# A graph layer on one core: slots ranked ahead, other segment lengths, a step's hand-overs moved, and a shorter last softplus

## The chip, the cores and the metric

The kernel runs on one core of one Trainium2 chip. Its time is that of one launch on the device, in microseconds, as the median of several runs. A core has five engines that run their own instruction streams in order and wait for each other through semaphores: TensorE (matmul, PE in the profile, its weight loads PEld), VectorE (DVE), ScalarE (ACT), GpSimd (POOL) and SyncE (SP), whose queue issues most of the transfers here.

## The reference

12,500 nodes with 128 features; 412,500 edges, sorted by their target `dst`, each with 20 edge attributes and a weight `rcut`. Layer norm and ReLU on the nodes, then one message-passing layer, then a residual:

```python
h = jnp.maximum(_layernorm(x, axis=-1), 0.0)
# the layer, with f_ij = edge_attr_20, rcut_ij = edge_weight, idx_i = src, idx_j = dst
h = h @ W_in2f
Wij = ssp(f_ij @ W_f1 + b_f1) @ W_f2 + b_f2        # ssp(x) = softplus(x) - log 2
Wij = Wij * rcut_ij[:, None]
x_ij = h[idx_j] * Wij
agg = jax.ops.segment_sum(x_ij, idx_i, num_segments=12500)
out = x + ssp(agg @ W_o1 + b_o1) @ W_o2 + b_o2
```

So rows of `h` are gathered by `dst`, which is sorted, and summed by `src`, which is not.

## The kernel before

Edges are taken in 806 chunks of 512, four chunks to a group, 202 groups. One step `k` of the main loop works on several chunks at once, and the code writes each engine's order out by hand (`tc.manual_schedule()`); the function `step` is that order. For a chunk there are these parts:

- `rows`: a window of 32 rows of `h`, split into three bf16 parts, is loaded (`near`), at a row number read from memory. It needs the rows of `h` to have been stored: they are made by `make_h`, four node tiles of 128 at a time (a quad), and the first quads are made ahead of and during the first steps.
- `hidden`, `hidden_log`, `hidden_end`: for a pair of chunks, the first matmul to `z` in PSUM, then softplus as Abs, Exp and Ln on ScalarE and a maximum-and-add on VectorE (L668), to `r`.
- `window`, `pick`, `picked`: a comparison builds a selection matrix `at` (L744), matmuls with `near` give the gathered rows (L772), and ScalarE scales them by `rcut` to `hg` (L780).
- `bias`, `value`: ScalarE writes the bias to `v` in PSUM (L757) and four f32 matmuls add `r @ wf2` to it (L764).
- `message`: VectorE multiplies `v` and `hg` into `o` (L791), and GpSimd issues four indirect DMAs (scatters) of 128 rows each (L795), to the slots found for these edges. `o` has four buffers of two chunks.
- `blocks`, `rank`, `rank_end`: the slots. A table in HBM has, for every block of 128 nodes, `T` tiles of 128 slots (one more in a part of the blocks); a running count in PSUM (`free`, L692 and L725) and a maximum over it (L697) give each edge a free slot of its block. This is done six chunks ahead (`LR`).

The edges are cut into segments, each with a table of its own, whose slots are cleared by DMA first (L1099). When a segment's edges are all scattered, it is collected: class `Collect` goes over the blocks in units of up to `UT` tiles, loads a unit (`m`, L833), compares places with slots (`to`, L844), sums by matmul into a PSUM bank `acc` (L857) and adds four blocks at a time to `agg` in SBUF (L880, `keep`). The collecting of all segments but the last is spread over the steps by a planner: a due time for each, and a rate of tiles a step, until six steps beyond the last chunk. The last segment is collected after the loop. With it the result is made for four blocks at a time (a node quad, 25 in all) by `finish`: `agg @ wo1` to PSUM (L414), softplus with Abs, Relu, Exp, Ln on ScalarE (L385 and others) and an addition on VectorE (L420), the bias added to the residual `xo` (L423), `@ wo2` (L427), the last addition (L431), and a store (L434).

Of the kernel before, what the change touches and what calls it, by code (L numbers as in the profile page):

```python
# [9 lines left out]
F32 = mybir.dt.float32  # L10
# [12 lines left out]
SEGS = (88, 40, 30, 14, 14, 8, 8)  # L23
# [6 lines left out]
UT = 6  # L30
# [11 lines left out]
def gnn_kernel(  # L42
# [38 lines left out]
    class Segment:  # L81
# [4 lines left out]
        def __init__(self, k):  # L86
# [7 lines left out]
            mean = (SEGS[k] * TG * P - (own[1] - own[0])) / QT * P / N  # L94
# [32 lines left out]


    tables = [(0, QN)]
# [4 lines left out]
    for c in range(NC):  # L134
        n = c * CH * N // n_edges
        table_of.append(0 if n < QN - NEAR - P else min(n // QN, NQ - 1) + 1)
# [4 lines left out]
    bf1, nbf1, bo1 = (sbuf(n, [P, 1]) for n in ("bf1", "nbf1", "bo1"))  # L141
# [10 lines left out]
    bf12 = sbuf("bf12", [P, P])  # L152
    zero = sbuf("zero", [P, ZR * RW])
# [27 lines left out]
    def load_x(q):  # L181
        n = min(QT, NTILE - q * QT)
        full = min(n, N // P - q * QT)
        xb = ln.tile([P, QT, P], F32, name="xb")
        if full < n:
            nc.vector.memset(xb[:, full:n, :], 0.0)
            nc.sync.dma_start(xb[:N % P, full, :], x[q * QN + full * P:N, :])
        if full:
            nc.sync.dma_start(xb[:, :full, :], x[q * QN:q * QN + full * P, :]
                              .rearrange("(c p) f -> p c f", p=P))  # L190
        return xb
# [59 lines left out]

    def constants():
# [3 lines left out]
        first_load(0)  # L256
        nc.sync.dma_start(win, w_in2f)

        for j in range(NCHUNK):
            nc.sync.dma_start(wf1[32 * j:32 * j + RBF, :], w_f1)  # L260

        nc.scalar.preload_act_table_set("natural_log_exp_and_others")
        nc.scalar.dma_start(bf1, b_f1[:, None])
        nc.scalar.dma_start(wf2, w_f2)
        nc.scalar.dma_start(bf2, b_f2[None, :].to_broadcast([P, P]))
        make_identity(nc, ident)
        for _ in bounds(0, nc.gpsimd):
            pass

        prow_i = early_room[:WP, rows_at + 5 * NC:rows_at + 5 * NC + 1].bitcast(I32)  # L270
# [6 lines left out]
                                pattern=[[1, P]], channel_multiplier=-1)  # L277
        nc.gpsimd.memset(zero, 0.0)
# [8 lines left out]
        nc.vector.memset(bad, 0.0)  # L287
        nc.vector.memset(rel[:, NPART - 1, :], 0.0)
        nc.vector.memset(ones, 1.0)
        nc.vector.memset(none, 0.0)  # L290

        for t in range(QT):
            nc.vector.memset(turn[:, :, t:t + 1], -1.0 if t % 2 else 1.0)
        nc.vector.tensor_scalar(prow_i, prow_i, 7, None, op0=ALU.logical_shift_right)
        nc.vector.tensor_copy(prow, prow_i)
# [3 lines left out]

    def biases(psum):  # L300

        nc.vector.tensor_scalar(nbf1, bf1, -1.0, None, op0=ALU.mult)
        b12 = psum.tile([P, QT, P], F32, name="b12", tag="acc")[:, 0, :]
        nc.tensor.matmul(b12, bf1.to_broadcast([P, P]), wf2, start=True, stop=True)
        nc.vector.tensor_add(bf12, b12, bf2)

    def late_loads():
        nc.sync.dma_start(wo1, w_o1)
        nc.sync.dma_start(wo2, w_o2)
        nc.sync.dma_start(bo1, b_o1[:, None])  # L310
        nc.sync.dma_start(bo2, b_o2[None, :].to_broadcast([P, P]))

    early = {}
    quads = []


    def make_h(q, psum):

        n = min(QT, NTILE - q * QT)
        xb = early.pop(q, None)  # L320
        if xb is None:
            xb = load_x(q)
            for _ in range(3):
                yield
# [39 lines left out]
        for (b, rows), table in zip(tables, h3_t):  # L364
            lo = max(0, b - q * QN) // P
            hi = min(n, (b + rows - q * QN) // P)
            if lo < hi:
                r = q * QN + lo * P - b
# [3 lines left out]
                if b + rows == QN:  # L372
                    yield
            if q == NQ - 1:
# [4 lines left out]
            h3[q * QN:q * QN + n * P, :].rearrange("(c p) f -> p c f", p=P),  # L379
            hb[:, :n, :, :].rearrange("p c k f -> p c (k f)"))  # L380
        yield
# [15 lines left out]
    def finish(t0, n, sT, quad, psum):  # L397
# [13 lines left out]
        yield  # L411

        z = psum.tile([P, 2, CH], F32, name="z_out", tag="z")[:, 0, :n * P]
# [3 lines left out]
        softplus_parts(a_n, r_n, z, bo1)  # L417
        softplus_logs(a_n)
        yield
        nc.vector.tensor_add(r_n, r_n, a_n)  # L420
        for p, cs, rows in pieces:
            xi = xo[:p, cs, :]
            nc.vector.tensor_add(xi, xi, spread(bo2[:p, :], xi.shape[1]))  # L423
        yield
        v = psum.tile([P, QT, P], F32, name="v_out", tag="v", bufs=3)
# [92 lines left out]
    with tc.tile_pool(name="edge", bufs=2) as edge, tc.tile_pool(  # L518
# [46 lines left out]
        class Group:  # L565


            def __init__(self, g):
# [3 lines left out]
                if g % NB == 0:  # L572
                    f = edge.tile([P, NB, CH], F32, name="f")
                    for j in range(NCHUNK):
                        nc.sync.dma_start(f[32 * j:32 * j + RBF, :, :],
                                          f_t[g:g + NB, j].rearrange("b k n -> k b n"))
                    kept["f"] = f
                self.f = kept["f"][:, g % NB, :]
                i = g - self.seg.g0
                if i % SB == 0:  # L580
                    w = min(SB, ceil_div(self.seg.c1, NCHUNK) - g) * TG
                    cols = slice(g * TG, g * TG + w)
                    src_i = edge.tile([P, SB * TG], I32, name="src_i")
                    nc.sync.dma_start(src_i[:, :w], src_t[:, cols])
                    rcut = edge.tile([P, SB * TG], F32, name="rcut")
                    nc.sync.dma_start(rcut[:, :w], rcut_t[:, cols])
                    kept["cols"] = [w, src_i, rcut]
                self.cols = kept["cols"]
                self.at = slice(i % SB * TG, (i % SB + 1) * TG)
                if g == 0:  # L590
                    rel_store(0)
                self.rel = edge.tile([WP, NCHUNK, CH], BF16, name="rel", bufs=4)
                nc.sync.dma_start(self.rel, rel_d[g * NCHUNK:(g + 1) * NCHUNK, :][None, :, :]
                                  .to_broadcast([WP, NCHUNK, CH]))
                self.inb = {}
                self.pair = {}
                self.near = {}

            def rows(self, c):

                k = self.g * NCHUNK + c
                t = table_of[k]
                i = int(k >= FIRST)
                at = k - heads[i].start
                self.near[c] = edge.tile([WP, P], BF16, name="near", bufs=8)
                start = nc.sync.value_load(shifts[i][0:1, at:at + 1], min_val=0,
                                           max_val=tables[t][1] - WR)
                nc.sync.dma_start(self.near[c], h3_t[t][bass.ds(start, WR), :]
                                  .rearrange("r (k f) -> (r k) f", f=P))

            def columns(self):
                if len(self.cols) == 3:
                    w, src_i, _ = self.cols
# [7 lines left out]
                    place = edge.tile([P, SB * TG], F32, name="place")  # L621
                    nc.vector.tensor_copy(place[:, :w], src_i[:, :w])

# [22 lines left out]
                self.rcut, self.blk, self.place, self.start = (t[:, self.at] for t in self.cols[2:])  # L646

            def hidden(self, c):

                z = psum.tile([P, 2, CH], F32, name="z")  # L650
                for k in range(2):
                    rows = slice(32 * (c + k), 32 * (c + k) + RBF)
                    nc.tensor.matmul(z[:, k, :], wf1[rows, :], self.f[rows, :],  # L653
                                     start=True, stop=True)
                a = quad.tile([P, 2, CH], F32, name="a", bufs=2)
                nc.scalar.activation(a, z, AF.Abs, bias=bf1)  # L656
                nc.scalar.activation(a, a, AF.Exp, scale=-1.0)  # L657
                self.pair[c] = z, a

            def hidden_log(self, c):  # L660
                _, a = self.pair[c]
                nc.scalar.activation(a, a, AF.Ln, bias=half, scale=0.5)  # L662

            def hidden_end(self, c):

                z, a = self.pair[c]
                r = quad.tile([P, 2, CH], F32, name="r")
                nc.vector.scalar_tensor_tensor(r, z, nbf1, a, op0=ALU.max, op1=ALU.add)  # L668
                self.pair[c] = r

            def blocks(self, c):
                inb = quad.tile([P, QT, NBLK], F16, name="inb")
# [6 lines left out]
            def rank(self, c):  # L679

                seg = self.seg
                if c == 0:
                    self.top = edge.tile([P, TG], F32, name="top")
                    self.slot = edge.tile([P, TG], I32, name="slot", bufs=4)
# [11 lines left out]
            def rank_end(self, c):  # L696
# [16 lines left out]
                if c == self.n - 1 or self.g == 0:  # L713

                    w = slice(c * QT if self.g == 0 else 0, (c + 1) * QT)
# [24 lines left out]

            def window(self, c):
# [6 lines left out]
            def bias(self, c):  # L748


                v = psum.tile([P, QT, P], F32, name="v", bufs=3)
                if self.g * NCHUNK + c < 2:
                    nc.tensor.matmul(v.rearrange("p t f -> p (t f)"),
# [458 lines left out]
```

## Time and profile before

| | |
|---|---|
| median of 3 runs | 4226.62 us (4223.92 to 4229.81) |
| the profiled execution itself | 5772.48 us |
| its span | 5770.8 us |
| mean granted TensorE clock | 0.718 |
| busy: PE, PEld, DVE, ACT, POOL | 67%, 50%, 59%, 47%, 54% |
| first scatter, start of the last scatter | 29.44 us, 5625.94 us |
| DMA | 820.8 MB, mean 142 GB/s |

The profiled execution is 37% longer than a run without the recorder. In rows of the trace the start comes first, then the duration in us, the engine, the line, the operation with output and inputs, and in brackets the idle time ahead of it and what ended it. In rows of groups the count, the busy time and the mean ns of one follow the names. In rows by stretch the engines follow as PE, PEld, DVE, ACT, POOL, then the granted clock, the DMA share and GB/s. PEclk among the slices is the granted clock in tenths.

### The profile page before, as it was taken

How to read it: one execution, taken by the hardware profiler on the slowest of the kernel's cores; microseconds unless marked ns; L12 is line 12 of the kernel's file. 1: busy time of each engine (PE TensorE's matmuls, PEld its weight loads, DVE VectorE, ACT ScalarE, POOL GpSimd, SP SyncE). 2: the span in 40 equal slices, each digit the busy share in tenths (PEclk: the TensorE clock that was granted, in tenths of full speed). 3: DMA queues.
4: the chain of work that ended last, by engine and by line, in shares of the span. 5: the costliest groups of instructions: out<-in, count | busy, mean ns of one | idle time of the engine just before them, and what ended most of it. 6: DMA issues, size and time to landing. Idle time of an engine off the chain costs nothing. (4 is left out here: it accounts for less than half of the span.)

```text
span 5770.8 us, 71871 instructions
## 1 busy us (share of the span) xinstructions
PE 3877.3 (67%) x21576; PEld 2912.2 (50%) x21576; DVE 3382.9 (59%) x6726; ACT 2715.3 (47%) x5490; POOL 3103.5 (54%) x3244
## 2 busy tenths in 40 slices
PE   5556555556555555577777777777777777777778
PEld 3333333333333333356655666566566665655557
DVE  5555555555444444466665666666666666566767
ACT  4455554555444444444444444444444444444444
POOL 5555555555555555555555555555555555555550
PEclk7665566565556566578777787788877788787879
DMA  5444443343333333255664554655555555555547
GB/s 150 138 135 141 130 141 119 115 137 104 99 89 87 106 109 87 82 152 161 188 183 137 158 160 144 190 163 157 160 168 173 154 150 178 165 141 153 145 126 215
DMA packets 515581, 820.80 MB, mean 142 GB/s; under 512 B 177074, under 2 KB 312870, under 8 KB 515186
## 3 DMA queue, kind: packets, MB, share of 16 engines
q1 hardware_dynamic: 411586, 602.85, 37.4%
q0 software_dynamic: 103168, 213.15, 11.2%
q8 instruction: 176, 2.88, 0.2%
q14 instruction: 219, 1.79, 0.1%
q10 hardware_dynamic: 432, 0.13, 0.0%
HBM read 419.09 MB, written 396.64 MB: 141 GB/s over the span
## 5 line engine op out<-in xcount | busy, mean ns | idle before, releaser
L795 POOL DMA_INDIRECT slots<-o,slot x3224 | 3100.3, 962 | 2522.6 <-DVE o L791 1605.2
L764 PE MATMUL v<-wf,r 128*128 128x128 f32 x6448 | 1209.4, 345 | 527.4 <-ACT a L657 207.3
L857 PEld LDWEIGHTS acc<-to,m 128*128 128x128 f32 x8132 | 1249.1, 238 | 577.1 <-issue 280.8
L857 PE MATMUL acc<-to,m 128*128 128x128 f32 x8132 | 1342.0, 329 | 271.0 <-DVE agg L880 136.4
L764 PEld LDWEIGHTS v<-wf,r 128*128 128x128 f32 x6448 | 1077.6, 251 | 850.7 <-issue 301.8
L780 ACT ACTIVATE hg<-picked,rcut 128x128 f32<-128x128 f32 x3224 | 913.1, 365 | 1256.6 <-remote 801.2
L697 DVE TENSOR_REDUCE top<-free 128x4 f32<-128x392 f32 x806 | 451.5, 560 | 1650.5 <-remote 990.2
L757 ACT ACTIVATE v<-bf 128x512 f32<-128x512 f32 x804 | 478.0, 595 | 1212.9 <-DVE o L791 888.5
L653 PE MATMUL z<-f,wf 20*128 20x512 f32 x1612 | 661.1, 881 | 406.9 <-DVE r L668 242.4
L844 DVE TENSOR_TENSOR to<-count_ps,m 128x512 f32<-128x512 f32 (+3 forms) x824 | 644.7, 806 | 255.3 <-remote 109.3
L772 PE MATMUL picked<-near,at 96*128 96x128 bf16 x3224 | 398.5, 257 | 495.3 <-ACT hg L780 317.4
L668 DVE SCALAR_TENSOR_TENSOR r<-z,nbf,a 128x1024 f32<-128x1024 f32 x403 | 516.2, 1281 | 242.3 <-ACT a L662 136.3
L656 ACT ACTIVATE a<-z,bf 128x1024 f32<-128x1024 f32 x403 | 454.0, 1127 | 400.4 <-remote 267.8
L772 PEld LDWEIGHTS <-at 96*128 96x128 bf16 x3224 | 315.5, 118 | 558.1 <-issue 531.3
L791 DVE TENSOR_TENSOR o<-v,hg 128x512 f32<-128x512 f32 x806 | 547.8, 680 | 16.8 <-ACT hg L780 12.8
L744 DVE TENSOR_TENSOR at<-count_ps,rel 96x512 bf16<-96x512 f32 x806 | 545.3, 677 | 0.0
L653 PEld LDWEIGHTS z<-f,wf 20*128 20x128 f32 x1612 | 174.6, 241 | 620.9 <-issue 428.9
L662 ACT ACTIVATE a<-a,half 128x1024 f32<-128x1024 f32 x403 | 468.1, 1162 | 0.0
L673 DVE TENSOR_TENSOR inb<-count_ps,blk 128x392 f16<-128x392 f32 x806 | 445.9, 554 | 0.0
L657 ACT ACTIVATE a<-a 128x1024 f32<-128x1024 f32 x403 | 425.8, 1057 | 12.8
L725 PE MATMUL free<-inb,rest_of 128*128 128x392 f16 x806 | 335.3, 416 | 117.6 <-issue 46.9
L692 PE MATMUL free<-inb,after 128*128 128x392 f16 x806 | 335.9, 417 | 17.4 <-issue 13.6
(108 smaller groups left out, 1142.5 us busy)
## 6 DMA issues: line engine op xcount, KB each, us to landing
m<-slots SPq DMA_DIRECT2D x311, 387.0 KB
m<-slots SPq DMA_DIRECT2D x317, 258.0 KB
rel<-rel_d SPq DMA_DIRECT2D x202, 384.0 KB
m<-slots SPq DMA_DIRECT2D x172, 322.5 KB
slots<-o,slot POOLq DMA_INDIRECT x3224
slots<-zero SPq DMA_DIRECT2D x96, 387.0 KB
slots<-zero SPq DMA_DIRECT2D x64, 516.0 KB
f<-in_f_t SPq DMA_DIRECT2D x404, 80.0 KB
```

The costliest lines, as they stand in the source:

```text
L653: nc.tensor.matmul(z[:, k, :], wf1[rows, :], self.f[rows, :], start=True, stop=True)
L662: nc.scalar.activation(a, a, AF.Ln, bias=half, scale=0.5)
L668: nc.vector.scalar_tensor_tensor(r, z, nbf1, a, op0=ALU.max, op1=ALU.add)
L744: nc.vector.tensor_tensor(at, prow_ps.to_broadcast([WP, CH]), self.rel[:, c, :], op=ALU.is_equal)
L757: nc.scalar.activation(v, spread(bf12, QT), AF.Copy)
L764: nc.tensor.matmul(v[:, i, :], r[:, i * P:(i + 1) * P], wf2, start=False, stop=True, skip_group_check=True)
L772: nc.tensor.matmul(ps[:, i, :], at[:, i * P:(i + 1) * P], near, start=i == 0, stop=i == QT - 1, skip_group_check=True)
L780: nc.scalar.activation(hg[:, i, :], ps[:, i, :], AF.Copy, scale=self.rcut[:, j:j + 1])
L791: nc.vector.tensor_mul(o[:, :, :P], v, hg)
L795: put = nc.gpsimd.indirect_dma_start(out=views[j % VIEWS], out_offset=bass.IndirectOffsetOnAxis(ap=self.slot[:, j:j + 1], axis=0), in_=o[: ...
L844: nc.vector.tensor_tensor(to[:, :n, :], count_ps[:, None, :].to_broadcast([P, n, P]), self.m[u][:, :n, P:].to_broadcast([P, n, P]), op=ALU ...
L857: nc.tensor.matmul(self.acc[b // QT][:, i, :], m[:, j, :P], to[:, j, :], start=t == 0, stop=t == self.seg.tiles(b) - 1)
```

## The change

- **Slots ahead.** What finds the slots leaves `Group` for a class `Places`. The lead of the ranks over the step ramps over 20 steps to 6, and from step 100 on grows by one every four steps to 64. In the last 64 steps no ranks are left, and the PSUM bank of the counts then serves as a second bank for the sums.
- **Segments.** Nine instead of seven; the last three have 3, 3 and 4 groups, so that one tile a block is enough for them. Units have up to 4 tiles (`UT`), `m` nine buffers. The planner counts 3.3 tiles more for the end of each quad and lets the last 64 steps take 1.3 times the work.
- **Hand-overs.** The order in a step is rewritten: the message goes first, the result of a rank is read a step later, picks are made two chunks ahead from step 18 on, Abs and Exp stand with Ln in the next step, the sums of a unit are added a step later, the sums of a quad are kept at several places of a step.
- **Bias.** The bias goes to `v` by a fifth matmul, from three bf16 parts of it, behind the four; `v` has one buffer, `picked` two, where both shared three.
- **First tile alone.** `make_h` takes tile 0, then tiles 1 to 3, then quads; a table of 128 rows serves the first chunks. Constants and small loads are put in another order.
- **Last softplus.** Abs, Exp and Ln; then one VectorE operation takes the maximum with `z` from PSUM and adds. The bias on `xo` is added by GpSimd. `bo1` is folded into `bo2` through a matmul made earlier.

The core of the diff:

```diff
-SEGS = (88, 40, 30, 14, 14, 8, 8)
+SEGS = (88, 41, 25, 18, 12, 8, 3, 3, 4)
+LEAD = 64
-UT = 6
+UT = 4
...
-            mean = (SEGS[k] * TG * P - (own[1] - own[0])) / QT * P / N
+            edges = min(n_edges, self.c1 * CH) - self.c0 * CH
+            mean = (edges - (own[1] - own[0])) / QT * P / N
...
+    made_h = [(0, 1), (1, QT - 1)]
+    made_h += [(t, min(QT, NTILE - t)) for t in range(QT, NTILE, QT)]
-    tables = [(0, QN)]
+    tables = [(0, P), (0, QN)]
...
@@ finish
+        for p, cs, rows in pieces:
+            xi = xo[:p, cs, :]
+            nc.gpsimd.tensor_add(xi, xi, spread(bo2[:p, :], xi.shape[1]))
...
-        softplus_parts(a_n, r_n, z, bo1)
+        nc.scalar.activation(a_n, z, AF.Abs, bias=bo1)
         softplus_logs(a_n)
         yield
-        nc.vector.tensor_add(r_n, r_n, a_n)
-        for p, cs, rows in pieces:
-            xi = xo[:p, cs, :]
-            nc.vector.tensor_add(xi, xi, spread(bo2[:p, :], xi.shape[1]))
-        yield
-        v = psum.tile([P, QT, P], F32, name="v_out", tag="v", bufs=3)
+        nc.vector.scalar_tensor_tensor(r_n, z, nbo1, a_n, op0=ALU.max, op1=ALU.add)
+        yield
+        v = psum.tile([P, QT, P], F32, name="v_out", tag=tag, bufs=bufs)
...
@@ value
+            def value(self, c):
+                v = psum.tile([P, QT, P], F32, name="v", bufs=1)
                 r = self.pair[c // 2 * 2][:, c % 2, :]
                 for i in range(QT):
                     nc.tensor.matmul(v[:, i, :], r[:, i * P:(i + 1) * P], wf2,
-                                     start=False, stop=True, skip_group_check=True)
+                                     start=i == 0, stop=False, skip_group_check=True)
+                nc.tensor.matmul(v.rearrange("p t f -> p (t f)"), ones_b, spread(bf12_p, QT),
+                                 start=False, stop=True, skip_group_check=True)
...
@@ collecting
-                m = edge.tile([P, UT, RW], F32, name="m", bufs=5)
+                m = edge.tile([P, UT, RW], F32, name="m", bufs=9)
+        def sums_tile():
+            kept["banks"] = kept.get("banks", 0) + (made["rank"] == NCH - 1 and not ranked)
+            if kept["banks"] % 2:
+                return state_ps.tile([P, QT, P], F32, name="acc_b", tag="free")
+            return psum.tile([P, QT, P], F32, name="acc")
...
+        RAMP = 20
+        LEAD_AT = 100
+        LATE = NCH - LEAD
+        def ahead(k):
+            lead = LR if k < LEAD_AT else min(LR + (k - LEAD_AT) // 4, LEAD)
+            return min(k + lead, k + 1 + (k + 1) * (LR - 1) // RAMP, NCH - 1)
...
@@ step, the new order
+            if not steady:
+                slots()
             if has(k):
                 g, c = of(k)
                 g.message(c, vs.pop(k), hgs.pop(k))
+            keep()
+            if steady:
+                slots()
+                if ahead(k) > made["rank"] + 1:
+                    rank()
+            else:
+                part("window", k + 1 + max(0, k) * 2 // (RAMP - 2), window)
+            if waiting():
+                add(2)
+            part("blocks", made["rank"] + 2, blocks, place)
+            part("end", min(k + LZ - 2 if steady else k + 1, made["log"]), pairs(hidden_end))
+            keep()
+            if steady:
+                part("window", k + 3, window)
...
+            part("pick", k + 1 if k < RAMP - 2 else k + 2, pick)
             if has(k + 1):
                 g, c = of(k + 1)
+                vs[k + 1] = g.value(c)
+            if waiting():
+                add(1)
+            for seg, u in units:
+                seg.load(u + AHEAD)
             if has(k + 1):
+                hgs[k + 1] = g.picked(c, ps.pop(k + 1))
...
+            part("log", min(k + LZ - 1, made["hidden"]), pairs(hidden_log))
+            keep()
             for c, u in units:
                 c.compare(u)
+                summed.append((c, u))
+            while made["rank"] < ahead(k):
+                slots()
+                rank()
             part("hidden", k + LZ, pairs(hidden))
...
+            if units:
+                add(len(units) if waiting() and units[-1][0].seg.T == 1 else 1)
...
@@ planner
+        def pace(k):
+            return k + 0.3 * max(0, k - LATE)
+        def cost(c, u):
+            return c.units[u][1] * c.units[u][3] + 3.3 * c.ends(u)
```

## The prediction

> **What bounds the kernel now.** I read the page's busy shares first: no engine is above 67%, so the bound is a rhythm, not a sum. The slices, the costliest group of GpSimd and its instructions in order of time show the rhythm:
>
> ```profile
> PE   5556555556555555577777777777777777777778
> POOL 5555555555555555555555555555555555555550
> PEclk7665566565556566578777787788877788787879
> L795 POOL DMA_INDIRECT slots<-o,slot x3224 | 3100.3, 962 | 2522.6 <-DVE o L791 1605.2
> ```
>
> ```profile
> 2210.29 0.96 POOL L795 DMA_INDIRECT slots<-o,slot  x1 [7.74 <-DVE o L791]
> 2211.55 0.96 POOL L795 DMA_INDIRECT slots<-o,slot  x1 [0.30 <-issue]
> 2212.82 0.96 POOL L795 DMA_INDIRECT slots<-o,slot  x1 [0.30 <-issue]
> ```
>
> A scatter takes 0.96 us and the next never starts sooner than 0.30 us later: 1.265 us apart, four to a step (one chunk of 512 edges), 5.06 us a step. The median step of chunks 200 to 400 sits on that floor; the others wait for VectorE's product (1605 us in total), mostly after pauses in which TensorE, VectorE and ScalarE all stand still for some microseconds.
>
> The profiled execution took 5772.5 us (span 5770.8, 1.7 around it), the runs shown 4226.6. First scatter at 29.4, start of the last at 5625.9: 5596.5 us, of which 3223 x 1.265 = 4077 is the floor and 1519 pauses. The timed runs have room for no pause: 4226.6 - 29.4 - 4077.1 = 120 us from the last scatter's start to the end. The profile has 146.6 there, but in 34.6 of these it still collects ten node quads of the last segment but one (VectorE's sums at 5629 to 5660.5); with four buffers of two chunks VectorE can run six chunks (30 us) ahead of GpSimd, and without pauses those quads lie under the scatters. 146.6 - 34.6 + 5 for landing and reloading the last rows = 117. So a timed run is **head 29 + floor 4077 + tail about 120**, and only what changes one of the three counts.
>
> The head, in order of time (six rows of many):
>
> ```profile
> 4.30 0.29 DVE L328 BATCH_NORM_STATS2 st<-xb 128x6 f32<-128x128 f32 x1 [0.71 <-DMA xb<-in_x]
> 16.05 0.39 SPq L369 DMA_DIRECT2D h<-hb  x1
> 20.48 0.59 PE L772 MATMUL picked<-near,at 96*128 96x128 bf16 x4
> 26.60 1.28 DVE L668 SCALAR_TENSOR_TENSOR r<-z,nbf,a 128x1024 f32<-128x1024 f32 x1 [6.46 <-ACT a L662]
> 28.47 0.68 DVE L791 TENSOR_TENSOR o<-v,hg 128x512 f32<-128x512 f32 x1
> 29.44 1.13 POOL L795 DMA_INDIRECT slots<-o,slot  x1 [25.45 <-DVE o L791]
> ```
>
> The first product could start at 22.2 (its `hg` is done), but VectorE stands in order before the second pair's `r`, which waits 6.5 us for ScalarE.
>
> One node quad of the tail on VectorE, and TensorE's share of such a stretch:
>
> ```profile
> 5684.61 0.69 DVE L880 TENSOR_TENSOR agg<-agg,acc 128x512 f32<-128x512 f32 x1
> 5685.22 0.68 DVE L420 TENSOR_TENSOR r_out<-r_out,a_out 128x512 f32<-128x512 f32 x1
> 5685.82 0.69 DVE L423 TENSOR_TENSOR xo<-xo,bo 128x512 f32<-128x512 f32 x1
> 5686.42 0.68 DVE L844 TENSOR_TENSOR to<-count_ps,m 128x512 f32<-128x512 f32 x1
> 5687.02 0.68 DVE L431 TENSOR_TENSOR xo<-xo,v_out 128x512 f32<-128x512 f32 x1
> 5687.62 0.68 DVE L844 TENSOR_TENSOR to<-count_ps,m 128x512 f32<-128x512 f32 x1
> 5688.35 0.69 DVE L880 TENSOR_TENSOR agg<-agg,acc 128x512 f32<-128x512 f32 x1
> ```
>
> ```profile
> 5680.00:5700.00 20.00, 19.98 (x140) 16.64 (x139) 19.67 (x33) 13.06 (x21) 0.00 (x0) 1.00 0.88 264
> ```
>
> Six VectorE operations at 0.60 us, 3.74 us a quad; TensorE 19.98, VectorE 19.67 of 20 us, DMA 264 GB/s at 0.88 busy: three resources full together.
>
> **Two pages of the skill.** "TensorE: Matmul & The Clock Gate", Part 1, says that the array runs at half clock unless it was busy over the last 3.4 us or so. The trace agrees: the same eight value matmuls take 2.07 us at a granted 0.5 and 1.06 at 1.0. So I price TensorE at full clock where its steps leave no such gap, and keep the half clock as a rival. "SBUF — State Buffer", Who interferes with whom, says that a VectorE operation with both inputs in SBUF and a GpSimd operation that reads SBUF exclude each other. No row shows that here. It bears on the bias addition that moves to GpSimd: of VectorE's four tail operations after the change each reads PSUM on one side (count, sums, z, v), so I charge nothing.
>
> **The change, part by part.**
>
> *Head.* One node tile instead of four goes through the normalisation: statistics -1.3, scaling -0.8, transposes -0.9, ReLU -0.4, product -1.5, three splits and two subtractions -1.8, load about -0.5 (durations of the rows above 16.05, three quarters off). The store leaves at about 9 instead of 16. The product also goes ahead of the second `r`. What is late next is the value branch: f landed 8.5, z 2.1, three ScalarE passes 3.35, `r` 1.3, value matmuls 2.1, product 0.7, about 18.5; and VectorE's own list before the product adds up to 15.9 us from 3.4 on, 19.3. First scatter at 20, bounds 17.5 and 25: **-9.4**.
>
> *First steps.* The first seven scatter steps take 6.25, 6.19, 5.06, 6.16, 6.10, 7.43, 5.06: 6.9 us over the floor, with two ranks a step. Slots now ramp over 20 steps. I take **-3** (0 to -7).
>
> *Hand-overs.* Rank results, log passes and picks are read a step later. They take waits out of steps that stand on the scatter floor: **0** in timed runs. `v` goes from a share of three buffers to one, so TensorE's value matmuls wait for the last product, the first thing in VectorE's step; behind them stand the adds and the hidden layer. The loop product 0.7 + value 1.0 (2.1 at half clock) + bias is under 3.4, below 5.06: 0. Between steps 100 and 332 a quarter more rank work: VectorE +0.35 us, TensorE +0.1 to 0.2, on steps with over 1 us free: 0.
>
> *Bias by matmul.* ScalarE loses 0.60 us a step (it has 3.3 of 5.06): 0. TensorE gains a 512-column bf16 matmul; nearest row, the 392-column f16 one, 0.17 us apart at full clock, so 0.22 (0.44 at half). See the budget below.
>
> *Segments.* By the kernel's own formulas tiles go from 4066 to 4182, loads of `m` from 824 to 1202 (units of 4, not 6), clears from 144 to 155 MB. SP: +378 issues at 0.34 us, 0.3 us on a queue that is busy 2.3 us a step: 0, with nine `m` buffers instead of five ahead. VectorE's budget moves little until step 780. TensorE per step at full clock: value 0.97, pick 0.36, ranks 0.34, hidden 0.53, collecting 0.24 a tile. Before: 8.5 tiles, 4.25 us. After: 8.5 tiles and bias, 4.5 to step 742; 10.4 tiles without ranks, 4.6 to step 780; 11.9 tiles, 4.95 in the last 26, where VectorE has 3.1 compares (1.9), 2.1 sums (1.3), and 1.9 for the rest, 5.1. Those 26 steps exceed the floor by 0 to 0.7 us, up to 18, and the 30 us that VectorE is ahead hides it. DMA there: 1.21 MB a step, 240 GB/s, below the 264 of the tail. **0**, up to +25 if the lead is gone.
>
> *Tail.* The last segment needs one tile a block: per quad one compare, one sum, one maximum-and-add from PSUM (0.69, as a 512-wide operation), one output addition: 4 x 0.60 + 0.1 = 2.5. TensorE 8 x 0.12 + 0.86 + 0.90 = 2.7. DMA 264 + 2 x 262 KB at 300 GB/s (264/0.88) = 2.63. ScalarE 2.04. The bias addition on GpSimd has no row; "GPSIMD Engine Reference", 3.1, gives 2.6 cycles an element at 1.2 GHz, an estimate of 1.1 us, under the quad's own time. I take 2.85 (bounds 2.7 and 3.3): 24 x (3.74 - 2.85) = **-21.4** (-10 to -25).
>
> Sum: -9.4 - 3 - 21.4 = -33.8. On the profiled execution that is 5772.5 to about 5739, if its pauses stay; on the median 4226.6 to **4193**, -0.8%.
>
> **Rivals.** *A, as above* (60%): 4193, own span 4172 to 4215. *C, the packed last steps* (14%): steps 780 to 805 slip by 0.7 to 1 us, the lead is spent and the remaining 16 quads show behind the last scatter: +20 to +35, 4213 to 4228. For it: VectorE's 5.1 us. *B, TensorE becomes the bound while collecting* (17%), the case that ends slower. In the trace the granted clock there is 0.78 and TensorE busy 77%:
>
> ```profile
> 3000.00:4000.00 1000.00, 766.24 (x4647) 613.42 (x4647) 619.97 (x1145) 464.34 (x938) 541.73 (x564) 0.78 0.54 158
> ```
>
> Before, 4.25 us pass into 5.06 down to a mean clock of 0.84; after, 4.5 only down to 0.89. At 0.86 it is +0.17 us on 387 steps, +0.27 on 38, +0.75 on 26: 66 + 10 + 20 = +96, so 4289. Against it: the clock falls in the pauses, which timed runs lack. *D, the floor of timed runs is lower than the profile's* (9%): if the 0.30 us gap is partly the recorder's and scatters come 1.24 apart, today's runs contain 80 us of waits in the steps, which the later hand-overs would take: down to 4115. *The change doing nothing*: if slots ahead bought only idle time, A's head and tail remain, since they are other edits.
>
> **Numbers.** About 0.2% (8.5 us) is what a measurement of this kernel can tell from no change. Faster: A, D and most of C, 0.77; within: the rest of C and a mild B, 0.07; slower: B, 0.16. The range 4150 to 4235 takes A, C, part of D and the mildest B, leaving about 2 in 10 out.
>
> **What would show it.** First scatter near 20 us; scatter starts still 1.265 apart; tail quads near 2.85 us with about 100 us from the last scatter's start to the end, less what is left over; TensorE under 5 us a step. Wrong if more steps than before stand above 5.06 with GpSimd waiting, or if the quads stay above 3.3.

## The result, and the profile after

The kernel after takes 4291.14 us (median of four runs, 4286.26 to 4292.98), the kernel before 4228.22 (4223.92 to 4230.60): a ratio of 1.0148, 95% interval 1.0131 to 1.0166, so 63 us slower. The forecast was 4193.

One thing has to be known to read the numbers: on some chips ("pausing") TensorE, VectorE and ScalarE stand still together again and again, so that before takes some 5725 to 5875 us there, timed or profiled, as in the profile ahead of the prediction, and on others ("steady") it takes 4224 to 4247 us; all comparisons below stay within one kind. This is before on a steady chip:

> The kernel before once more, for a profile on a chip where it takes 4228 us (on the last chip it took 5729 us and showed the same pauses as the first profile). Theory 1: without the pauses its first 20 steps take under 115 us (139 in the kernel after), its steps from 650 to 780 are at the scatters' floor (5.2 us in the kernel after) and the tail from the last scatter's start takes about 117 us (112 after). Theory 2 (rival B): its steps are at the floor all along and so are those of the kernel after, which leaves only a wider scatter spacing: 1.265 here against 1.272. If the spacing is 1.272 here too, the spacing belongs to the chip and not to the change.

It took 4236.7 us (span 4234.9), the timed runs beside it 4226.8 to 4242.4. The page of after, the lines that answer those shown of before: span, slices of TensorE and GpSimd, granted clock, the scatters.

```profile
span 4289.6 us, 75606 instructions
...
PE   5776776777666666679988998989988888889987
...
POOL 4677777777777777777777777777777777767772
PEclk7777778777787778789999999999999999899999
...
L854 POOL DMA_INDIRECT slots<-o,slot x3224 | 3123.0, 969 | 1052.7 <-issue 758.4
```

and the same lines of before from a steady chip (before_b):

```profile
span 4234.9 us, 71871 instructions
...
PE   7777776677777777788888888888888888888878
...
POOL 5777777777777777777777777777777777777760
PEclk8776667766666666679999999999999999999999
...
L795 POOL DMA_INDIRECT slots<-o,slot x3224 | 3095.9, 960 | 1011.6 <-issue 793.5
```

GpSimd is the engine to read. It is at its rhythm in both kernels (its slices are level, most of its idle time is the 0.30 us of "issue"), yet the same 3224 scatters are busy 27 us longer. The rest is found by laying the starts of the scatters in order and taking sections. Step `k` begins with the first of chunk `k`'s four scatters. Each row is worked out from the scatter rows of the traces; the columns are one profiled execution each on steady chips, and the last four are explained under the experiments.

| us | before | after | end_early_b | ee_xo9_vec_c | segs_vec_b | spread |
|---|---|---|---|---|---|---|
| start of the first scatter | 29.7 | 21.7 | 21.7 | 21.7 | 21.7 | 21.7 |
| median step | 5.050 | 5.086 | 5.086 | 5.051 | 5.051 | 5.050 |
| 805 median steps | 4065.3 | 4094.2 | 4094.2 | 4066.1 | 4066.1 | 4065.3 |
| above that, steps 0 to 20 | 3.3 | **37.5** | 4.2 | 6.4 | 4.0 | 6.6 |
| steps 20 to 700 | 8.3 | 6.6 | 4.6 | 4.9 | 4.0 | 5.6 |
| steps 700 to 760 | 0.1 | **15.8** | 8.6 | **25.1** | 0.0 | 0.9 |
| steps 760 to 805 | 0.0 | 0.0 | 0.0 | -0.1 | 0.0 | 0.0 |
| three scatters left in the last step | 3.8 | 3.8 | 3.8 | 3.8 | 3.8 | 3.8 |
| last scatter's start to the end | 124.4 | 109.9 | 114.0 | 101.7 | 124.2 | 100.7 |
| span | 4234.9 | 4289.6 | 4251.2 | 4229.6 | 4223.8 | 4204.6 |

From before to after: -8.0 at the head, +29 in the length of a scatter, +34 in the first 20 steps, +16 around step 730, -2 in the steps between, -14.5 at the end; together +54.7 of span. The head and the end are what the change was forecast to bring; three other losses outweigh them.

The head of after, in order of time (six rows of many):

```profile
2.92 0.29 DVE L359 BATCH_NORM_STATS2 st<-xb 128x6 f32<-128x128 f32 x1 [1.95 <-DMA xb<-in_x]
15.88 1.28 DVE L804 SCALAR_TENSOR_TENSOR r<-z,nbf,a 128x1024 f32<-128x1024 f32 x1
17.21 2.08 PE L819 MATMUL v<-wf,r 128*128 128x128 f32 x8 [0.73 <-DVE r L804]
19.85 0.86 DVE L375 TENSOR_SCALAR xb<-xb,mv,rs 128x128 f32<-128x128 f32 x3
20.70 0.68 DVE L850 TENSOR_TENSOR o<-v,hg 128x512 f32<-128x512 f32 x1
21.68 1.13 POOL L854 DMA_INDIRECT slots<-o,slot  x1 [16.61 <-DVE o L850]
```

The value matmuls end at 19.3, but VectorE then stands in the normalisation of tiles 1 to 3 (19.85) before it comes to the product.

VectorE in a quad at the end, first as it should run, then 40 us later:

```profile
4208.21 0.68 DVE L949 TENSOR_TENSOR agg<-agg,acc_b 128x512 f32<-128x512 f32 x1
4209.04 0.75 DVE L459 SCALAR_TENSOR_TENSOR r_out<-z_out,nbo,a_out 128x512 f32<-128x512 f32 x1
4209.71 0.68 DVE L913 TENSOR_TENSOR to<-count_ps,m 128x512 f32<-128x512 f32 x1
4210.31 0.68 DVE L467 TENSOR_TENSOR xo<-xo,v_out 128x512 f32<-128x512 f32 x1
4210.90 0.68 DVE L949 TENSOR_TENSOR agg<-agg,acc 128x512 f32<-128x512 f32 x1
...
4241.15 0.69 DVE L913 TENSOR_TENSOR to<-count_ps,m 128x512 f32<-128x512 f32 x1 [3.21 <-DMA m<-slots]
...
4247.24 0.69 DVE L913 TENSOR_TENSOR to<-count_ps,m 128x512 f32<-128x512 f32 x1 [0.17 <-DMA m<-slots]
...
4251.26 0.69 DVE L913 TENSOR_TENSOR to<-count_ps,m 128x512 f32<-128x512 f32 x1 [0.58 <-DMA m<-slots]
```

Four operations and 2.69 us a quad (4208.21 to 4210.90) at first; from about 4214 on most compares wait for their `m`, and quads come mostly 3.5 to 4 us apart. In the stretches of after at the end (us, busy time of TensorE, its loads, VectorE, ScalarE, GpSimd, clock, share of the DMA engines, GB/s) no engine is full then, nor are the DMA engines:

```profile
4200.00:4215.00 15.00, 15.00 (x105) 12.56 (x104) 14.10 (x23) 11.46 (x17) 2.54 (x2) 1.00 0.69 193
4215.00:4285.00 70.00, 51.96 (x305) 40.13 (x303) 42.64 (x69) 32.76 (x50) 21.12 (x18) 0.95 0.68 192
```

### The profile page after: what moved, and what is told of

Its sections match the earlier page's. It is cut to its first block, busy times and chain, and to the rows that moved or that the text cites. A ratio compares the mean times of both kernels' runs of the same rounds, so it can differ in the third digit from the quotient of the medians.

```text
span 4289.6 us, 75606 instructions
## 1 busy us (share of the span) xinstructions
PE 3426.0 (80%) x22612; PEld 2589.0 (60%) x22612; DVE 3425.3 (80%) x7238; ACT 2315.9 (54%) x4670; POOL 3158.3 (74%) x3276
## 3 DMA queue, kind: packets, MB, share of 16 engines
q0 software_dynamic: 103168, 213.15, 14.5%
## 4 chain that ended last, share of the span: by engine, by line
## 5 line engine op out<-in xcount | busy, mean ns | idle before, releaser
L819 PE MATMUL v<-wf,r 128*128 128x128 f32 x6448 | 1069.2, 317 | 266.7 <-DVE o L850 264.9
L819 PEld LDWEIGHTS v<-wf,r 128*128 128x128 f32 x6448 | 933.7, 223 | 301.7 <-DVE o L850 293.3
L926 PEld LDWEIGHTS acc<-to,m 128*128 128x128 f32 x7484 | 941.3, 202 | 225.9 <-issue 128.4
L926 PE MATMUL acc<-to,m 128*128 128x128 f32 x7484 | 998.8, 289 | 36.0 <-DVE to L913 29.9
L788 PE MATMUL z<-f,wf 20*128 20x512 f32 x1612 | 529.5, 737 | 224.4 <-DVE r L804 223.5
L913 DVE TENSOR_TENSOR to<-count_ps,m 128x512 f32<-128x512 f32 (+2 forms) x1202 | 673.7, 607 | 23.3 <-DMA m<-slots 23.0
L804 DVE SCALAR_TENSOR_TENSOR r<-z,nbf,a 128x1024 f32<-128x1024 f32 x403 | 514.0, 1275 | 23.0 <-ACT a L797 22.5
L848 DVE COPY o<-place 128x8 f32<-128x8 f32 x403 | 78.9, 196 | 482.7 <-DMA slots<-o,slot 482.0
L830 PEld LDWEIGHTS <-at 96*128 96x128 bf16 x3224 | 264.4, 107 | 241.0 <-issue 88.0
L788 PEld LDWEIGHTS z<-f,wf 20*128 20x128 f32 x1612 | 138.4, 210 | 400.3 <-DVE r L804 339.7
L830 PE MATMUL picked<-near,at 96*128 96x128 bf16 x3224 | 350.6, 237 | 17.7 <-DVE at L810 16.5
L821 PE MATMUL v<-bf_p,ones_b 128*128 128x512 bf16 x806 | 351.0, 435 | 0.0
```

The costliest lines, as they stand in the source:

```text
L819: nc.tensor.matmul(v[:, i, :], r[:, i * P:(i + 1) * P], wf2, start=i == 0, stop=False, skip_group_check=True)
L830: nc.tensor.matmul(ps[:, i, :], at[:, i * P:(i + 1) * P], near, start=True, stop=True)
L913: nc.vector.tensor_tensor(to[:, :n, :], count_ps[:, None, :].to_broadcast([P, n, P]), self.m[u][:, :n, P:].to_broadcast([P, n, P]), op=ALU ...
L926: nc.tensor.matmul(self.acc[b // QT][:, i, :], m[:, j, :P], to[:, j, :], start=t == 0, stop=t == self.seg.tiles(b) - 1)
```

## The experiments

In all, "floor" is the median step, and what lies above it is summed as in the table. Kernels with `ee` in the name carry the edit of the first experiment.

### The first 20 steps

The wait view of after, steps 0 to 20 (engine, line, what it waited for: us in total, times, longest):

```profile
POOL slots L854 <- DVE o L850: 58.3, 15, 16.6
...
PEld z L788 <- DVE r L804: 40.0, 11, 5.7
PE z L788 <- DVE r L804: 35.1, 11, 5.4
```

and of before_b, where 25.7 us are the head:

```profile
POOL slots L795 <- DVE o L791: 29.9, 5, 25.7
```

`z` has one buffer. A hidden layer's matmul (L788) waits until VectorE has made `r` (L804) of the pair before, and the value matmuls of the next step stand behind it on TensorE. The new order has a condition here: from step 20 on `r` is made up to chunk `k + 2`, in the first 20 steps only to `k + 1`; before, it was `k + 2` throughout. One such step of after, in order of time:

```profile
93.77 0.69 DVE L850 TENSOR_TENSOR o<-v,hg 128x512 f32<-128x512 f32 x1 [1.43 <-ACT hg L839]
...
95.45 1.27 DVE L804 SCALAR_TENSOR_TENSOR r<-z,nbf,a 128x1024 f32<-128x1024 f32 x1
...
96.78 2.05 PE L788 MATMUL z<-f,wf 20*128 20x512 f32 x4 [4.54 <-DVE r L804]
...
103.18 2.02 PE L819 MATMUL v<-wf,r 128*128 128x128 f32 x8
...
105.73 0.69 DVE L850 TENSOR_TENSOR o<-v,hg 128x512 f32<-128x512 f32 x1 [1.17 <-PE v L821]
```

TensorE idles 4.5 us, then works at a granted clock of 0.54 (mean of 96 to 106 us; eight value matmuls in 2.02 us; the Trainium skill, "TensorE: Matmul & The Clock Gate", Part 1, states such a gate after idle time), and the product comes 12 us after the one before. The edit takes the condition away:

```diff
-            part("end", min(k + LZ - 2 if steady else k + 1, made["log"]), pairs(hidden_end))
+            part("end", min(k + LZ - 2, made["log"]), pairs(hidden_end))
```

> The kernel after with r made two chunks ahead in the first 20 steps too, on a chip without the pauses. Theory 1: first 20 steps 102 to 115 us instead of 139, time 4255 to 4266. Rival (half clock, ranks and early tiles make the first steps slow): 4285 to 4295.

Measured: 4258.32 us (4252.93 to 4263.11), 1.0063 of before (1.0044 to 1.0081): 24 us over the before timed beside it, where after is 63 over its own. The same waits in that kernel:

```profile
POOL slots L854 <- DVE o L850: 22.2, 7, 16.6
...
PE z L788 <- DVE r L804: 11.7, 10, 2.3
```

Of the 58 us that GpSimd waited for products 36 are gone (16.6 is the head in both), and 4.2 us are left above the floor in place of 37.5. This loss is one line. The half clock by itself is not it: end_early_b is granted 0.51 in the same stretch, 96 to 106 us, and its steps there stand on the floor.

### The length of a scatter

The bias addition to `xo` put back on VectorE, in a kernel that also has nine `xo` buffers (next section); and before with its index tiles elsewhere:

```diff
-            nc.gpsimd.tensor_add(xi, xi, spread(bo2[:p, :], xi.shape[1]))
+            nc.vector.tensor_add(xi, xi, spread(bo2[:p, :], xi.shape[1]))
```

> As ee_xo9, and the addition of the output bias to the rows of x is on VectorE again, not on GpSimd. Theory S1: the scatters of the kernel after take 967 ns where those of before take 958 because GpSimd's program now also holds an arithmetic instruction of another kind; then the median falls back to 958 ns, the spacing to 1.263 us, and the time is about 29 us under ee_xo9 less what VectorE loses at the end (24 quads of 0.7 to 0.9 us, some 17 to 21 us where VectorE is the bound): 4225 to 4245. Theory S2: it comes from where the tiles of indices and messages lie, or from the program's size; then 967 ns stays, and the time is 10 to 20 us over ee_xo9.

```diff
-                    self.slot = edge.tile([P, TG], I32, name="slot", bufs=4)
+                    self.slot = edge.tile([P, TG], I32, name="slot", bufs=22)
```

> The kernel before with 22 buffers for the tiles of scatter indices in place of 4, nothing else: the indices and all tiles behind them lie elsewhere in SBUF, and an index tile is used again 22 groups later instead of 4. If a scatter's 967 ns in place of 958 comes from where its index tile lies, scatters here last 963 to 967 ns, and the time is 15 to 29 us over before. If not, 958 ns and the time of before, 4228 to 4240 us.

Both fell on a pausing chip, where whole times don't show it (5298.17 us, 0.9216 of before, 0.9175 to 0.9256; before_slot22 5759.86), but the durations do. The instruction of GpSimd by itself (ns min/median/max): ee_xo9, which has the addition on GpSimd, then ee_xo9_vec.

```profile
L854 POOL DMA_INDIRECT slots<-o,slot x386: 962/968/1027, 2000.0 to 2599.1; - x193
```

```profile
L854 POOL DMA_INDIRECT slots<-o,slot x385: 952/958/1017, 2000.0 to 2599.1; - x193
```

968 ns with the addition in GpSimd's program, 958 without it, on one chip; before_slot22 has 958 too on that chip, so moving the index tiles alone doesn't make scatters longer. Does the whole get shorter without the addition? On a steady chip:

> First hidden layers a step later, nine buffers for x, the bias on VectorE, on a chip where before takes 4228 to 4240 us if it can be had. With 958 ns for a scatter every step at its floor is 0.036 us shorter than in end_early_b, 29 us over 805 steps; the last stretch is 105 to 115 us (end_early_b 114): VectorE takes the addition back (7 to 20 us), SyncE waits less for stores (0 to 12). So 4222 to 4240 us. If the 29 us do not show in the whole, some other thing sets the step: 4250 or more.

Measured: 4222.30 us (4217.27 to 4231.42, ten runs), 0.9974 of before (0.9964 to 0.9983). Its median scatter lasts 958 ns, its median step is 5.051 us instead of 5.086: 28 us over 805 steps, as the table shows. The 26 additions all run behind the scatters, as in after:

```profile
4179.71 0.97 POOL L854 DMA_INDIRECT slots<-o,slot  x1 [0.30 <-issue]
4182.44 1.27 POOL L447 TENSOR_TENSOR xo<-xo,bo 128x512 f32<-128x512 f32 x1 [1.75 <-DMA xo<-in_x]
```

So nothing shares GpSimd with the scatters in time. These are longer from the start (median of the first 40: 967 ns in after, 958 in before_b). The median over a run is 967 to 971 ns in the nine profiles with that instruction in the program, 958 to 962 in the eleven without it. It isn't the chip: on one and the same chip before_b, segs64 and spread have 958, end_early_b 967. Why an instruction that hasn't run yet costs the others 9 ns each is not shown, nor whether its kind or the length of the program counts. The Trainium skill, "GPSIMD Engine Reference", 2.1, says that a small program on GpSimd looks up each instruction's kind and calls its code; it doesn't say that a further kind makes the others slower, and no run here looks inside.

### SyncE behind its stores

SyncE's own waits at the end of after:

```profile
SPq L443 <- DMA out<-xo: 43.3, 19, 4.3
SPq L470 <- DVE xo L467: 13.3, 5, 7.3
```

With six buffers a load of `xo` waits 19 times, 43 us in all, for an earlier store from the same buffer to land, and the loads of `m` stand behind it on SyncE's queue: between 4230 and 4242 us SyncE waits three times, 6.7 us, for such stores, and issues one load of `m` after each. The compares' waits for `m` fit that. Nine buffers, alone:

```diff
-        xo = quad.tile([P, QT, P], F32, name="xo", bufs=6)
+        xo = quad.tile([P, QT, P], F32, name="xo", bufs=9)
```

> The kernel after with nine buffers for the residual tiles of the tail instead of six. Theory: the tail's node quads come 3.6 us apart instead of 2.7, since the load of a residual tile waits on SyncE's queue for a store to land and the load of the slots stands behind it; with nine buffers they come about 2.7 us apart over 16 quads, -10 to -15 us, 4276 to 4281. Rival: the quads are held by what the DMA engines deliver (0.65 busy in that stretch); then the time stays within 4 us of 4291.

On a pausing chip 5287.5 us, 0.9173 of before (0.9146 to 0.9201): no faster than end_early beside it, which has six buffers and the first edit (5288.0, 0.9185, 0.9164 to 0.9206). SyncE's largest wait at the end, in end_early and then in xo9, where no wait of L443 is left:

```profile
SPq L443 <- DMA out<-xo: 44.2, 19, 4.3
```

```profile
SPq L470 <- DVE xo L467: 34.9, 22, 9.5
```

The stretch behind the last scatter is 107.4 us where end_early has 128.4; the first 20 steps, without the first edit, are 12 us slower. So the edit does in its place what was expected; the whole doesn't show it. With both edits:

> The kernel after with two edits: the hidden layers of the first steps collected a step later as in all later steps (as in end_early_b), and nine buffers for the rows of x in place of six. If the last stretch is held by SyncE's loads of x that wait until an earlier store of the same buffer has landed (43.3 us of waits, 19 times, in the kernel after), it shortens: from the last scatter to the end some 98 to 104 us in place of the 114 of end_early_b, and the time is 4244 to 4250 us, 10 to 14 us under end_early_b. If the loads are held by the traffic itself, it stays at 4255 to 4263.

Again a pausing chip: 5280.8 us, 0.9185 (0.9148 to 0.9222), 107.9 us behind the last scatter; with the bias on VectorE (ee_xo9_vec) 114.9. On a steady chip nine buffers were measured only together with the bias on VectorE: 101.7 us where end_early_b has 114.0. The DMA engines were not at their limit in after: there they move 192 GB/s at 0.68 busy, in ee_xo9_vec_c 225 at 0.82 (4163 to 4225 us).

### The short segments

Ranks run 64 chunks ahead from step 332 on, so the ends of segments, by `SEGS`, come at about steps 672, 704, 716, 728 and 742 in after, at 680, 712 and 742 with the segments of before. VectorE has extra work at each: a new segment's columns and a check of the old one. In order of time, around step 728 of after:

```profile
3771.92 0.68 DVE L850 TENSOR_TENSOR o<-v,hg 128x512 f32<-128x512 f32 x1
...
3773.65 0.55 DVE L728 COPY used<-free 1x392 f32<-1x392 f32 x1 [0.58 <-PE free L722]
3774.24 0.55 DVE L734 TENSOR_REDUCE ext<-used 1x1 f32<-1x388 f32 x1
...
3776.35 0.14 DVE L736 TENSOR_SCALAR bad<-ext 1x1 f32<-1x1 f32 x1
...
3779.17 1.87 DVE L913 TENSOR_TENSOR to<-count_ps,m 128x512 f32<-128x512 f32 x3
3780.96 0.68 DVE L850 TENSOR_TENSOR o<-v,hg 128x512 f32<-128x512 f32 x1
```

The check alone takes from 3773.65 to 3776.49, the product comes 9.0 us after the one before, and the columns stood in the step ahead of it. A product need not be in time by itself: VectorE runs ahead of GpSimd, by a median of 27 us between steps 100 and 650 in after and never less than 18.6 (start of the scatter less start of its product). That lead is 18 us at step 680, 12 at 710, 4 at 720, and 1 at 730: then each late product shows.

The segments of before, in ee_xo9_vec_c:

> As ee_xo9_vec_c with the seven segments of before. If the checks and the columns of the three short segments make the 8.6 us over the steady step between steps 700 and 760 of end_early_b, 0 to 4 us are left there and the whole is some 5 to 9 us under ee_xo9_vec_c less what the longer last segment costs behind the last scatter (0 to 20 us). 4215 to 4235 us if it costs little, 4235 to 4255 if it costs the 20.

```diff
-SEGS = (88, 41, 25, 18, 12, 8, 3, 3, 4)
+SEGS = (88, 40, 30, 14, 14, 8, 8)
```

Measured, on the chip of ee_xo9_vec_c: 4227.90 us (0.9983, 0.9976 to 0.9990). Above the floor 0.0 us between steps 700 and 760 for 25.1, with the lead never under 9 us; behind the last scatter 124.2 for 101.7. In these two profiles the short segments lose around step 730 what they save at the end; by the medians they are still 5.6 us ahead. From the product of step 700 to that of step 730 VectorE is busy 150.8 us with the short segments and 138.4 with the old ones; the columns and the checks of the two ends more make some 11 us of the difference.

Then two ways to keep the short end, both as edits of ee_xo9_vec_c: fewer segment ends, or the same work given out in small pieces.

> The kernel ee_xo9_vec_c with last segments of 6 and 4 groups in place of 3, 3 and 4. One segment end and one set of columns less: 6.2 us less of VectorE's work around steps 716 to 740, with what waits for it 8 to 13 us of the 25; a last segment of 4 groups as before, so the stretch behind the last scatter stays at about 102 us: 4208 to 4216 us. If the 6 groups, now collected in the last 16 steps, are too much for these: the lead of 14 to 24 us at steps 780 to 805 is spent and the end comes 5 to 20 us later, 4220 to 4235.

```diff
-SEGS = (88, 41, 25, 18, 12, 8, 3, 3, 4)
+SEGS = (88, 41, 25, 18, 12, 8, 6, 4)
```

Measured: 4221.43 us (0.9975, 0.9966 to 0.9984). 8.8 us above the floor in steps 700 to 760 instead of 25.1, 105.7 behind the last scatter instead of 101.7: its profile is 11 us under that of ee_xo9_vec_c, but the medians are equal within their intervals, so a gain in the whole isn't shown. The time falls where the second theory put it, but not by its cause: the lead isn't spent at the end (24.8 us at step 805).

> The kernel ee_xo9_vec_c, and the checks at the end of a segment (seven to nine instructions of VectorE, some 4 us in the step in which the segment's last rank is read) are put off and given out one to a step. Theory: VectorE's products run 27 us ahead of GpSimd at step 600, lose that over steps 650 to 720, and what is lost after that (25 us over the floor between steps 700 and 760) are checks and new columns that stand in a step all at once. The same work spread loses less to waiting: 8 to 18 us over the floor, 4205 to 4216 us. If it is the sum of VectorE's work in those steps and not its lumps, 20 to 25 us stay: 4218 to 4226.

```diff
+            def limit(self, *args):
+                checks.append(lambda: self.limit_now(*args))
...
             part("log", min(k + LZ - 1, made["hidden"]), pairs(hidden_log))
+            if checks:
+                checks.pop(0)()
```

Measured: 4207.15 us (4199.55 to 4213.43), **0.9941 of before (0.9918 to 0.9964)**, the fastest kernel of the study. 0.9 us are left above the floor. GpSimd's waits for products between 3600 and 3840 us, in ee_xo9_vec_c and in spread (whose lines stand six further down):

```profile
POOL slots L854 <- DVE o L850: 29.4, 16, 4.6
```

```profile
POOL slots L860 <- DVE o L856: 2.1, 4, 1.0
```

The work is the same; only the lumps of the checks are gone, the columns stand as before. The lead is 26 us at step 700 (14 in the profile of ee_xo9_vec_c) and just lasts: 1.5 us at step 745. So it was the lumps of the checks. The medians are 15 us apart, the profiles 25: the profiled execution of ee_xo9_vec_c was the longest of its ten, so its 25.1 is a high value; the same segments left 8.6 in end_early_b and 15.8 in after.

### The other runs

All on pausing chips. The first two shared a chip with xo9; the first is the kernel before:

> The kernel before, unchanged, for a profile without the pauses of the first one, to set beside the kernel after. The kernel after has its first scatter at 21.7 us, takes 139 us over its first 20 steps (floor 102), 5.09 us a step from step 20 to 650, 5.2 from 650 to 780, and 112 us from the last scatter's start to the end. Theory 1 (the loss lies in the first 20 steps, in a slightly wider spacing of the scatters and in a tail that gains little): here the first 20 steps take under 115 us, scatters come 1.265 us apart, and the tail takes about 117 us. Theory 2 (TensorE became the bound while collecting, rival B of the prediction): here steps 361 to 780 are at the floor and the rest of the kernel is like the kernel after, first steps and spacing too.

5729.49 us; the timed runs beside it take as long (5755.49 median), so the pauses are not the recorder's. end_early, the edit of the first experiment: 5288.0 us, which says nothing of its edit, as after itself was not timed on a pausing chip. Two had the seven old segments: oldsegs (nothing else changed) 5240.3 us, 0.9105 (0.9082 to 0.9128), and

> As ee_xo9, with the seven segments of before (the last ones of 14, 8 and 8 groups). Theory: the ends of the three short segments, each with its check and its new columns on VectorE within 36 steps, cost the 9 to 16 us over the steady step between steps 700 and 760; with the old segments that is 0 to 4 us there, and a last segment of 8 groups instead of 4 makes the stretch behind the last scatter longer by at most 20 us, or by nothing where the quads set its pace. If the first part outweighs it: 4235 to 4245 us; if the second does: 4250 to 4265. Its scatters last 967 ns under either.

5243.16 us, 0.9115 (0.9070 to 0.9161). On these chips the old segments are faster, by 0.7% (ee_xo9_segs against ee_xo9), and where that comes from shows in the last 25 steps: 6.4 to 6.6 us a step in the four kernels with old segments, 7.7 to 7.9 with the new. The sections between steps 700 and 760 can't be read under pauses. ee_xo9, ee_xo9_vec and ee_xo9_segs were run again under new names (ee_xo9_b, ee_xo9_vec_b, and ee_xo9_segs_vec, which has the bias on GpSimd in spite of its name), together with segs_vec, the kernel of segs_vec_b, and met a pausing chip again: 5365.81, 5375.22, 5326.17 and 5354.62 us with before at 5855.78. There the old segments gain 0.7% (ee_xo9_segs_vec, one run) and 0.4% (segs_vec). The scatters take 971 ns with the addition on GpSimd and 962 without it, in two profiles each.

## Why the prediction was wrong, point by point

The model held: head, 3224 scatters at a fixed distance, end. Its count for before was 29.4 + 4077 + 120, and the unpaused profile has 29.7, 1.263 us a scatter and 124.4. What failed were terms of the change that were set to nothing or to a small gain.

- **Head, -9.4: right.** -8.0. The value matmuls end at 19.3, where 18.5 was worked out, and VectorE's list ahead of the product, put at 19.3, ends at 20.7 with the scaling of three tiles in it: 21.7 instead of 20, inside the bounds.
- **First steps, -3 (0 to -7): wrong, +34.** The forecast took from the ramp that slots cost less, and put the new order of hand-overs at 0. One condition of the diff makes `r` a step *later* than before in those 20 steps, and no term of the sum held what waits for it: the next hidden layer's matmul and, behind it on TensorE, the values. I priced the new order by its description and the steady branch. end_early_b shows nearly all of it (37.5 to 4.2). Nor were there 7 us to gain: without pauses these steps of before stand 3.3 us above the floor.
- **Spacing 1.265, unchanged: wrong, +29.** The floor was taken as given by the kind of instruction. The addition on GpSimd was priced at GpSimd's own time in the tail, and at that well enough ("GPSIMD Engine Reference", 3.1, an estimate of 1.1 us; measured 1.27). Its cost lay in 3224 other instructions at 9 ns each. The exclusion in "SBUF — State Buffer", Who interferes with whom, for which I charged nothing, does not show: VectorE's addition L467 lasts 677 ns in after, with GpSimd's beside it, and 668 in ee_xo9_vec_c and 716 in spread without (medians).
- **Segments, 0, "up to +25 if the lead is gone": the bound was right, the place and the value were not.** +16 in the profile of after. I counted tiles and TensorE's work and looked at the last 26 steps. The lead goes between steps 650 and 720, by checks and columns of segment ends that no term of the sum held; spread shows it for the checks, for the columns it is argued from VectorE's busy time.
- **Tail, -21.4 (-10 to -25): sign and bound right.** -14.5. VectorE's four operations and 2.69 us a quad are there for five quads of 25; then SyncE's loads behind its stores set the pace. I had priced each engine and the traffic, not the number of `xo` buffers. That the term still lay within its bounds was luck: the pace of most quads is one that it had not priced. With nine buffers it is -23 even with the bias on VectorE, five operations and 3.05 us a quad in most of them.
- **The bias by matmul, 0, and the later hand-overs: right.** In a stretch of 700 us of after

```profile
2600.00:3300.00 700.00, 628.39 (x4714) 514.03 (x4713) 622.73 (x1255) 378.43 (x761) 532.28 (x551) 0.96 0.76 230
```

  and of before (before_b)

```profile
2600.00:3300.00 700.00, 605.48 (x4524) 510.39 (x4524) 606.40 (x1144) 438.04 (x896) 530.97 (x555) 0.92 0.78 233
```

  TensorE goes from 4.37 to 4.57 us a step (busy share times the median step), +0.2 as estimated, and steps 200 to 650 stand at 5.09 on average, on their floor.
- **Rivals.** B named 4289, within 2 us of the result, by coincidence, and is refuted: the clock is 0.96, not 0.86, and the steps while collecting are on the floor. C did not happen on steady chips: the last 25 steps of after are at 5.09 with 18 to 24 us of lead. On pausing chips those steps are 1.2 to 1.5 us longer with the new segments than with the old. D fell: in before_b scatters stand 1.263 us apart, and that profiled execution took no longer than the timed runs beside it. And the pauses, which the prediction took for the profiler's, are the chip's; so are the 37% between the profile and the runs of the table.

Take away the three losses and the stores' wait, and most of the forecast's sum returns: spread lies 30.3 us of span under before_b, 24 us by the medians, where 33.8 was forecast; -8.0 of it is the head and -23.7 the end. It has the bias on VectorE, so it isn't the change as forecast.

## What to carry to other kernels

Where an engine's identical instructions set the time, watch their duration to the nanosecond: 9 ns on each of 3224 cost more than the head saved, and they came with a new instruction on that engine that ran only behind them. Read every condition of a changed order for the steps in which it is false, and ask for each hand-over whether it came earlier or later than before. Engines that run ahead hide late work only as long as the lead lasts: add up rare work (segment ends, checks) against the lead where it comes in clusters, and give it out in pieces before cutting it.

## What the runs showed of the hardware that was not expected

- An addition of 512 columns in GpSimd's program lengthens its indirect scatters, from medians of 958 to 962 ns to 967 to 971, from the start, before any addition has run.
- Chips differ: the same before takes 4224 to 4247 us on some and some 5725 to 5875 on others, with pauses common to three engines (123 stretches of over 2 us with all three idle in the profile of before, 10 in before_b) and a mean granted clock of 0.72 for 0.82. Kernels with the change are 8 to 9% *faster* than before on the latter (0.9105 to 0.9216) and from 0.6% faster to 1.5% slower on the former. Why they lose less to pauses is open, and so is what makes a chip pause.
- A load that reuses a buffer whose store is still under way can hold the queue behind it for up to 4.3 us at a time.
